# A graph attention layer on one core: ScalarE loads fifteen gathered chunks row by row, six rows with each group of sums

## The chip, the core and the metric

The kernel runs on one core of one Trainium2 chip. A core has five engines, each with its own queue of instructions that it works off in order: TensorE (PE in the profile; its weight loads are PEld), VectorE (DVE), ScalarE (ACT), GpSimd (POOL) and SyncE (SP), which here only issues transfers. They meet through semaphores. Transfers between the chip's memory and the core's on-chip memory (SBUF, 128 partitions) are issued by SyncE, ScalarE or GpSimd and carried out by 16 DMA engines. TensorE writes to PSUM, the accumulator memory. The metric is the device time of one execution in microseconds (us).

## The reference, cut to what matters

```python
h = jnp.maximum(_layernorm(x, axis=-1), 0.0)            # 12500 nodes x 128
# 200000 edges (src, dst), sorted by dst; 4 heads of 32
hn = (h @ W_node.T).reshape(num_nodes, H, HD)
e = (edge_attr_64 @ W_edge.T).reshape(num_edges, H, HD)
att_in = jnp.concatenate([hn[src], hn[dst], e], axis=-1)
att = jnp.sum(att_in * a, axis=-1)
att = jnp.where(att > 0, att, 0.2 * att)
m = jnp.maximum(jax.ops.segment_max(att, dst, num_segments=num_nodes), 0.0)
ex = jnp.exp(att - m[dst])
denom = segment_sum(ex, dst) + (num_edges - deg)[:, None] * jnp.exp(-m)
w = ex / denom[dst]
return x + segment_sum(w[:, :, None] * hn[src], dst).reshape(num_nodes, 128)
```

For each edge the transformed row of its source node is needed. That is the gather on which this document turns: 200000 rows of 137 numbers, 548 bytes each.

## The kernel before, in words

**Stages.** First the nodes are normalised and multiplied by the weights; the rows go to a table in the chip's memory (137 numbers a node: four heads of 32 with a one each, a count, four source logits). Then the edges are worked through in order of their targets.

**Tiling of the edges.** A *chunk* is 128 edges, one a partition. A *group* is four chunks: 511 edges and one place (partition 0 of chunk 0) that carries the sums of the group before. A *quad* is four groups, sixteen chunks. There are 392 groups and 98 quads. Quads are bundled into supers (two quads each at first, then four, then three and two at the end), and the softmax is done once for a super.

**Gathers.** `gather` (L136 to L149) issues one indirect DMA a chunk on GpSimd (L147): 128 rows of the table at 128 source indices, into `ga`. `ga_all` (L130) is a ring of eight quads, so the gathers of quad q need the sums of quad q - 8 to be closed. Quads 0 to 3 and half of quad 4 are gathered from the raw input `x` while the table is still being made.

**By-row chunks.** For some quads the last chunk of the last group is not gathered by GpSimd. `by_row` (L133) lists them: quads 16, 24, ... 96, eleven in all. For these `loaded_by_row` (L701 to L724), a generator that other code steps through, has ScalarE issue 128 small transfers of one row each, into a tile of its own. The source indices come in by a small load (`sources_of`), VectorE scales them to byte addresses (L713), and `windows` (L494) loads sixteen of these addresses at a time into ScalarE's registers (L496). Then come the row transfers (L722). When the logits of that quad are opened, ScalarE copies the tile into `ga` (in `all_logits`, L859).

**The chain of groups.** `sums` (L783) does the following for each group. VectorE weighs the gathered rows (L804) and marks which target each edge has (L817); TensorE multiplies chunks 1 to 3 (L822). Then `complete` closes the *previous* group by `complete_group` (L740 to L763), which is the place of the change:

1. VectorE multiplies the previous group's carried sums into partition 0 of `ga` (L745, the carry);
2. ScalarE copies the carried count (L749, the count copy);
3. the row generator is stepped;
4. TensorE multiplies chunk 0 and so closes the sums (L751);
5. ScalarE copies the closed sums out of PSUM (L752, the copy `pt`);
6. the row generator is stepped again.

The next carry (L745) waits for that copy. One step of the generator issues three rows or one in turn (it pauses ahead of rows p with p % 4 equal to 0 or 3), so a group sends three rows behind the count and one behind the sums, from the first quad on; 1408 rows take 352 groups. The load of the next sixteen addresses stands in the step behind the sums.

**Beside it.** The logits of quads further on (`open_logits`, `all_logits`; L556 to L565) and the softmax of the next super are interleaved with the sums. SyncE fetches the edge features (`ea`), targets (`db`), windows of target logits (`pw`) and of inputs (`xw`) ahead, and writes the results. `add_sources` (L586) is the first to need all gathers of a quad.

Of the kernel before, what the change touches and what calls it, by code (L numbers as in the profile page):

```python
# [15 lines left out]
P = 128  # L16
# [8 lines left out]
R_CNT, R_SRC, ROW = H * HW, H * HW + 1, H * HW + 5  # L25

J = 4
# [4 lines left out]
QG = 4  # L32
# [4 lines left out]
AT_ONCE = 4  # L37
RAW, MORE = 4, 2
QUADS = 8
AHEAD, EVERY = 16, 8  # L40
SETS = max(NODE_T, QG * J)
PAD = 1 << 20

# [1 line left out]
def blocks(total, step):  # L45
    return [(i, min(step, total - i)) for i in range(0, total, step)]
# [3 lines left out]
def kernel(  # L50
# [35 lines left out]
    nc = tc.nc  # L86
# [8 lines left out]
    table = dram.tile([NP, ROW], F32, name="table")  # L95
# [27 lines left out]
    quads = blocks(G, QG)  # L123
    nq = len(quads)
# [5 lines left out]
    ga_all = consts.tile([P, QUADS, QG, J, ROW], F32, name="ga")  # L130
    GA, GATHERED = {}, set()
    whole = lambda g: E - g * NE + 1 >= GE
    by_row = [q for q in range(AHEAD, nq, EVERY) if quads[q][1] == QG and whole(quads[q][0] + QG - 1)]  # L133
    is_by_row = lambda q, i, j: q in by_row and (i, j) == (QG - 1, J - 1)

    def gather(q, rows, width, lo, hi):  # L136
# [26 lines left out]
    with tc.manual_schedule():  # L163
# [6 lines left out]
        for _ in range(AT_ONCE):  # L170
            q, i = early.pop(0)
# [301 lines left out]
    with tc.tile_pool(name="work", bufs=2) as work, \  # L473
# [20 lines left out]
        def windows(of, size, g, n, engine=mybir.EngineType.SP):  # L494

            return nc.values_load_multi_w_load_instructions(  # L496
                of[0:1, g:g + n], engines=[engine], min_val=0, max_val=(N - 1) * size,
                skip_runtime_bounds_check_because="a node's row")[1]

        as_bytes = lambda d: d.bitcast(U8)  # L500
        rows_at = lambda d, at, size, n=SPAN: as_bytes(d.rearrange("n c -> (n c)"))[
            bass.ds(at, n * size)].rearrange("(n c) -> n c", c=size)
# [196 lines left out]
        ROW_TILES = {}  # L699

        def loaded_by_row():  # L701

            def sources_of(q):
                g = quads[q][0] + QG - 1
                of = work.tile([1, P], I32, name="of")
                nc.sync.dma_start(of, src.rearrange("(o e) -> o e", o=1)[:, (g + 1) * GE - P:(g + 1) * GE])
                return of

            of = sources_of(by_row[0]) if by_row else None
            yield  # L710
            for k, q in enumerate(by_row):
                at_row = work.tile([1, P], I32, name="at_row")
                nc.vector.tensor_scalar(at_row, of, float(4 * ROW), None, op0=OP.mult)  # L713
                tile_q = work.tile([P, ROW], F32, name="by_row")
                for p0 in range(0, P, QG * J):
                    if p0 == P // 2 and k + 1 < len(by_row):
                        of = sources_of(by_row[k + 1])
                    at = windows(at_row, 4 * ROW, p0, QG * J, mybir.EngineType.Activation)
                    for p in range(QG * J):
                        if p % J in (0, J - 1):  # L720
                            yield
                        nc.scalar.dma_start(as_bytes(tile_q[p0 + p:p0 + p + 1, :]),  # L722
                                            rows_at(table, at[p], 4 * ROW, 1))
                ROW_TILES[q] = tile_q  # L724

        row_steps = loaded_by_row()
        next(row_steps)

# [3 lines left out]
        def complete():  # L732

            division = None if "held" in state else state.pop("division", None)
            if begun:
                complete_group(*begun.pop())
            if division:
                divide(*division)

        def complete_group(q, i, ga, hot, pt, acc, fc):  # L740
            g0, m = quads[q]
            g = g0 + i
            if g:
                before = state["before"]
                nc.vector.tensor_tensor(  # L745
                    ga[0:1, i, 0, 0:H * HW].rearrange("p (h w) -> p h w", w=HW),
                    before[WIN:WIN + 1, 0:H * HW].rearrange("p (h w) -> p h w", w=HW),
                    fc.unsqueeze(2).to_broadcast([1, H, HW]), op=OP.mult)
                nc.scalar.copy(ga[0:1, i, 0, R_CNT:R_CNT + 1], before[WIN:WIN + 1, R_CNT:R_CNT + 1])  # L749
                next(row_steps, None)  # L750
            nc.tensor.matmul(acc, hot[:, i, 0, :], ga[:, i, 0, :], start=False, stop=True)  # L751
            nc.scalar.copy(pt[:, i, :], acc)  # L752
            state["before"] = acc
            next(row_steps, None)

            parts = {nq - 1: (2, 3), nq - 2: (2,), nq - 3: (2,)}.get(q, ())
            if i + 1 in parts or i == m - 1:
                lo = max([k for k in parts if k <= i], default=0)
                den = work.tile([SPAN, QG, H], F32, name="den")
                nc.scalar.activation(den[:, lo:i + 1, :], pt[0:SPAN, lo:i + 1, R_SRC:R_SRC + H],  # L760
                                     AF.Exp, scale=-1.0)
                state["division"] = q, pt, den, lo, i + 1
# [413 lines left out]
```

## Time and profile before

| | |
|---|---|
| median of 3 runs | 2010.57 us (2009.75 to 2010.74) |
| the profiled execution | 2015.4 us, span 2013.6 us from first to last instruction |
| mean granted TensorE clock | 0.54 |
| bytes moved | 279.70 MB, mean 139 GB/s |

Times of single instructions come from that one profiled execution. In the profile a line of a group gives the source line, the engine, the operation, the tile written and read, the count, then the busy time and the mean duration, then the idle time of the engine just ahead of these instructions and what ended it. A line of the timeline gives the start and the length in us, and in brackets the idle time ahead with its releaser. A line of waits gives who waited, for whom, how long in all, how often, and the longest. ACTq and SPq are the queues of ScalarE and SyncE: issuing a DMA there keeps the queue, but is not counted as busy time of the engine.

### The profile page before, as it was taken

The numbers are of one execution on the slowest core, as the hardware profiler recorded it, in microseconds if no ns is written. First come the engines' busy times: TensorE is split into PE (matmuls) and PEld (weight loads), VectorE is DVE, ScalarE is ACT, GpSimd is POOL, SyncE is SP. The second block draws the span as 40 slices with busy tenths as digits, with TensorE's granted clock in tenths as the row PEclk, the third lists the DMA queues.
The fourth block names the chain that finished last, engine by engine and source line by source line (L and its number), as shares of the span: only waits on it lengthen the run. The fifth ranks groups of instructions, "written<-read, shape, count | busy, mean of one in ns | idle before, by whom it ended". The sixth has DMA issues, their size and how long they took to land. (4 is left out here: it accounts for less than half of the span.)

```text
span 2013.6 us, 30145 instructions
## 1 busy us (share of the span) xinstructions
PE 1383.0 (69%) x7317; PEld 1253.6 (62%) x7317; DVE 1323.0 (66%) x3272; ACT 420.1 (21%) x1542; POOL 1500.1 (74%) x1598
## 2 busy tenths in 40 slices
PE   6587798775766666657666666667575766777775
PEld 5576788765665556656656565566565655666665
DVE  7674788774775766656747655657476565677776
ACT  6664112111111111111111111111111111122122
POOL 7777677777777777777777777777777777777774
PEclk8766555555555555555555555555555555555557
DMA  7654666655566555555555555565555554555541
GB/s 252 204 145 110 156 157 155 162 138 129 134 151 147 133 131 138 135 132 142 128 133 134 136 131 147 122 146 124 136 133 135 133 145 121 138 153 138 134 102 36
DMA packets 196601, 279.70 MB, mean 139 GB/s; under 512 B 81092, under 2 KB 145999, under 8 KB 188584
## 3 DMA queue, kind: packets, MB, share of 16 engines
q1 hardware_dynamic: 142150, 165.56, 30.5%
q0 software_dynamic: 49760, 108.84, 24.0%
q10 hardware_dynamic: 4514, 3.36, 0.7%
q8 instruction: 61, 1.00, 0.2%
q14 instruction: 116, 0.95, 0.2%
HBM read 254.25 MB, written 23.30 MB: 138 GB/s over the span
## 5 line engine op out<-in xcount | busy, mean ns | idle before, releaser
L147 POOL DMA_INDIRECT ga<-table,srci x1483 | 1412.9, 953 | 463.5 <-issue 386.4
L822 PE MATMUL acc<-ga,hot 128*97 128x137 f32 x2352 | 644.8, 445 | 67.9 <-ACT ga L797 29.8
L822 PEld LDWEIGHTS acc<-ga,hot 128*97 128x97 f32 x2352 | 513.3, 276 | 89.0 <-ACT ga L797 48.1
L562 PEld LDWEIGHTS <-at 80*128 80x128 bf16 x1568 | 213.2, 164 | 483.6 <-DVE at L556 465.1
L562 PE MATMUL lg<-pw,at 80*128 80x12 bf16 x1568 | 169.3, 181 | 409.5 <-DVE at L556 405.4
L565 PE MATMUL lg<-wblk,ea 128*128 128x8 f32 x1568 | 407.2, 357 | 0.0
L565 PEld LDWEIGHTS lg<-wblk,ea 128*128 128x128 f32 x1568 | 379.7, 307 | 0.0
L586 DVE TENSOR_TENSOR U<-st,ga 128x64 f32<-128x64 f32 x98 | 26.4, 269 | 413.4 <-DMA ga<-table,srci 403.3
L556 DVE TENSOR_TENSOR at<-const_ps,db 80x512 bf16<-80x512 f32 x392 | 267.3, 683 | 5.8
L804 DVE TENSOR_TENSOR ga<-ga,ex_ps 128x528 f32<-128x528 f32 x392 | 268.4, 685 | 0.6 <-issue 0.3
L751 PE MATMUL acc<-ga,hot 128*97 128x137 f32 x784 | 257.4, 431 | 3.8 <-ACT ga L749 3.7
L752 ACT COPY pt<-acc 97x137 f32<-97x137 f32 x392 | 107.4, 274 | 717.1 <-PE acc L751 655.4
L745 DVE TENSOR_TENSOR ga<-acc,facs 1x132 f32<-1x132 f32 x391 | 115.8, 296 | 132.3 <-ACT pt L752 122.2
L751 PEld LDWEIGHTS acc<-ga,hot 128*97 128x97 f32 x784 | 197.7, 281 | 6.6 <-ACT ga L749 6.5
L817 DVE TENSOR_TENSOR hot<-const_ps,slot 128x320 f32<-128x320 f32 x384 | 183.2, 477 | 0.0
L749 ACT COPY ga<-acc 1x1 f32<-1x1 f32 x391 | 59.9, 153 | 430.6 <-DVE ga L745 408.3
L147 POOL DMA_INDIRECT ga<-in_x_dram,srci x72 | 68.8, 956 | 23.4 <-issue 17.7
L845 DVE TENSOR_TENSOR res<-pt,const_ps 80x512 f32<-80x512 f32 (+2 forms) x102 | 67.5, 662 | 3.8 <-DVE const_ps L841 0.3
L849 DVE TENSOR_TENSOR res<-res,xw 80x512 f32<-80x512 f32 (+2 forms) x99 | 66.8, 675 | 3.4
L404 PE MATMUL row_ps<-wcat,hT 128*128 128x137 f32 x198 | 40.9, 358 | 20.5 <-DVE tgt L410 10.7
L624 ACT ACTIVATE low<-t_ps 64x511 f32<-64x511 f32 (+2 forms) x28 | 16.5, 589 | 176.3 <-PE t_ps L622 176.3
L678 PE MATMUL ex_ps<-ident,ex 64*128 64x64 f32 (+2 forms) x112 | 18.5, 313 | 49.1 <-ACT ex L665 49.1
(139 smaller groups left out, 1045.1 us busy)
## 6 DMA issues: line engine op xcount, KB each, us to landing
db<-in_dst_dram SPq DMA_DIRECT2D x98, 640.0 KB
ea<-in_edge_t_dram SPq DMA_DIRECT2D x98, 512.0 KB
ga<-table,srci POOLq DMA_INDIRECT x1483
by_row<-table ACTq DMA_DIRECT2D x1408, 0.5 KB
xw<-in_x_dram SPq DMA_DIRECT2D x392, 40.0 KB
out_dram<-res SPq DMA_DIRECT2D x392, 40.0 KB
pw<-side SPq DMA_DIRECT2D x392, 1.9 KB
table<-row SPq DMA_DIRECT2D x9, 616.5 KB
```

The costliest lines, as they stand in the source:

```text
L147: nc.gpsimd.indirect_dma_start(out=ga[:, i, j, 0:width], out_offset=None, in_=rows, in_offset=bass.IndirectOffsetOnAxis(ap=srci[:, g0 + i, ...
L556: nc.vector.tensor_tensor(at[:, i, :], node_ps[0:SPAN, g0 + i:g0 + i + 1].to_broadcast([SPAN, GE]), db[:, i, :], op=OP.is_equal)
L562: nc.tensor.matmul(lg[:, i, j].rearrange("p k h -> p (k h)"), at[:, i, j * P:(j + 1) * P], sw, start=i + j == 0, stop=False, skip_group_ch ...
L565: nc.tensor.matmul(lg[:, i, 2 * w:2 * w + 2, 0, :], ea[:, i, w, :], wblk, start=False, stop=True, skip_group_check=True)
L745: nc.vector.tensor_tensor(ga[0:1, i, 0, 0:H * HW].rearrange("p (h w) -> p h w", w=HW), before[WIN:WIN + 1, 0:H * HW].rearrange("p (h w) -> ...
L751: nc.tensor.matmul(acc, hot[:, i, 0, :], ga[:, i, 0, :], start=False, stop=True)
L752: nc.scalar.copy(pt[:, i, :], acc)
L804: nc.vector.tensor_tensor(val, val, weight.unsqueeze(3).to_broadcast([P, J, H, HW]), op=OP.mult)
L817: nc.vector.tensor_tensor(hot[:, i, :, 0:SPAN], lane_ps.unsqueeze(1).to_broadcast([P, J, SPAN]), slot[:, g, :].unsqueeze(2).to_broadcast([ ...
L822: nc.tensor.matmul(acc, hot[:, i, j, :], ga[:, i, j, :], start=j == 1, stop=False)
L845: nc.vector.tensor_tensor(res[:, :n, :].rearrange("p g (h d) -> p g h d", d=HD), val[:, :, :, 0:HD], share_ps[0:R, :n, :].unsqueeze(3).to_ ...
L849: add.tensor_tensor(res[:, :n, :], res[:, :n, :], xw, op=OP.add)
```

## The change

`by_row` is set from other constants, the generator yields after every row, and `complete_group` steps it five times behind the count and once behind the sums, from quad 6 on. The addresses are loaded twelve at a time. The fifteen by-row quads are 21, 26, 31, 37, 42, 47, 53, 58, 63, 69, 74, 79, 85, 90 and 95.

```diff
-AHEAD, EVERY = 16, 8
+ROWS_FROM, ROWS_AHEAD = 6, 9
+BEHIND_COUNT, BEHIND_SUMS, LOADED = 5, 1, 12
...
-    by_row = [q for q in range(AHEAD, nq, EVERY) if quads[q][1] == QG and whole(quads[q][0] + QG - 1)]
+    by_row = [ROWS_FROM + ROWS_AHEAD - -(k + 1) * P // ((BEHIND_COUNT + BEHIND_SUMS) * QG) for k in range(nq)]
+    by_row = [q for q in by_row if q < nq and quads[q][1] == QG and whole(quads[q][0] + QG - 1)]
...
-                for p0 in range(0, P, QG * J):
-                    if p0 == P // 2 and k + 1 < len(by_row):
+                for p in range(P):
+                    if p == P // 2 and k + 1 < len(by_row):
                         of = sources_of(by_row[k + 1])
-                    at = windows(at_row, 4 * ROW, p0, QG * J, mybir.EngineType.Activation)
-                    for p in range(QG * J):
-                        if p % J in (0, J - 1):
-                            yield
-                        nc.scalar.dma_start(as_bytes(tile_q[p0 + p:p0 + p + 1, :]),
-                                            rows_at(table, at[p], 4 * ROW, 1))
-                ROW_TILES[q] = tile_q
+                    if p % LOADED == 0:
+                        at = windows(at_row, 4 * ROW, p, min(LOADED, P - p), mybir.EngineType.Activation)
+                    nc.scalar.dma_start(as_bytes(tile_q[p:p + 1, :]),
+                                        rows_at(table, at[p % LOADED], 4 * ROW, 1))
+                    if p == P - 1:
+                        ROW_TILES[q] = tile_q
+                    yield
+
+        def load_rows(q, n):
+
+            for _ in range(n if q >= ROWS_FROM else 0):
+                next(row_steps, None)
...
                 nc.scalar.copy(ga[0:1, i, 0, R_CNT:R_CNT + 1], before[WIN:WIN + 1, R_CNT:R_CNT + 1])
-                next(row_steps, None)
+                load_rows(q, BEHIND_COUNT)
             nc.tensor.matmul(acc, hot[:, i, 0, :], ga[:, i, 0, :], start=False, stop=True)
             nc.scalar.copy(pt[:, i, :], acc)
             state["before"] = acc
-            next(row_steps, None)
+            load_rows(q, BEHIND_SUMS)
```

## The prediction

> **What bounds the kernel now.** I read the page's busy shares and costliest groups first, then GpSimd's own instructions in order of time, then who waits for whom, stage by stage.
>
> ```profile
> span 2013.6 us, 30145 instructions
> PE 1383.0 (69%) x7317; PEld 1253.6 (62%) x7317; DVE 1323.0 (66%) x3272; ACT 420.1 (21%) x1542; POOL 1500.1 (74%) x1598
> L147 POOL DMA_INDIRECT ga<-table,srci x1483 | 1412.9, 953 | 463.5 <-issue 386.4
> L147 POOL DMA_INDIRECT ga<-in_x_dram,srci x72 | 68.8, 956 | 23.4 <-issue 17.7
> ```
>
> No engine looks full: GpSimd (POOL) leads with 74%. Its busy time is the issue of 1483 + 72 = 1555 indirect gathers, one per 128 edges; the question is what its idle quarter is.
>
> ```profile
> 1009.55 0.94 POOL L147 DMA_INDIRECT ga<-table,srci  x1 [0.30 <-issue]
> 1010.79 0.94 POOL L147 DMA_INDIRECT ga<-table,srci  x1 [0.30 <-issue]
> ...
> 1969.23 0.94 POOL L147 DMA_INDIRECT ga<-table,srci  x1 [0.30 <-issue]
> ```
>
> The gathers stand back to back, 1.25 us from start to start: 0.94 of work and 0.30 that belongs to no wait. Who released GpSimd between 260 us and its last gather, and the group of these gathers, say the same for the whole stretch:
>
> ```profile
> POOL ga L147 <- issue: 354.7, 1163, 0.3
> POOL ga L147 <- PE acc L822: 29.9, 98, 0.3
> POOL ga L147 <- DMA ga<-table,srci: 14.6, 48, 0.3
> L147 POOL DMA_INDIRECT ga<-table,srci x1360 | 1296.3, 953 | 414.7 <-issue 354.7 <-PE acc L822 29.9 <-DMA ga<-table,srci 14.6
> ```
>
> The longest "wait" is 0.3 us whatever its releaser, so these are the fixed gap and no waits. One gather costs (1296.3 + 414.7) / 1360 = 1.258 us, and for 1360 gathers in a row nothing else sets GpSimd's pace. VectorE stands on the other side of that bound:
>
> ```profile
> L586 DVE TENSOR_TENSOR U<-st,ga x38: 266/267/325, 1018.9 to 1760.6; 128x64 f32<-128x64 f32 x38
>   DMA ga<-table,srci: 211.5, 33
> ```
>
> From 1000 to 1780 us L586, which needs a whole quad's gathers, waits 211.5 us for them over 38 quads: 5.6 us a quad in which VectorE, and what follows it, has nothing to do. That is the **cover** for anything the change adds to the group chain. Before 260 us it is different:
>
> ```profile
> POOL ga L147 <- PE acc L751: 11.2, 5, 5.8
> 255.73 0.94 POOL L147 DMA_INDIRECT ga<-table,srci  x1 [5.76 <-PE acc L751]
> ```
>
> From 150 to 260 us GpSimd waits five times for the closing matmul of an old group (L751), which frees a buffer of gathered rows: 11.2 - 5 x 0.3 = 9.7 us that it loses. After its last gather, 2013.6 - 1969.2 = 44.4 us of softmax, sums and results remain.
>
> **The change part by part.** *Fewer gathers.* Eleven by-row chunks become fifteen (the by-row quads are 21, 26, 31, 37 and so on to 95), so 1555 gathers become 1551. Four gathers at 1.258 us: -5.0 us. All lie ahead of GpSimd's last gather, so where they stand does not matter while GpSimd is the bound; the tail behind it keeps its length.
>
> *No rows for quads 0 to 5.* ScalarE used to issue rows from the first sums on, in the stretch where GpSimd waits for L751.
>
> ```profile
> 164.83 2.46 ACTq L722 DMA_DIRECT2D by_row<-table  x3
> 164.96 0.78 PE L751 MATMUL acc<-ga,hot 128*97 128x137 f32 x2
> 167.33 0.27 ACT L752 COPY pt<-acc 97x137 f32<-97x137 f32 x1 [2.42 <-DMA db<-in_dst_dram]
> ...
> ACT pt L752 <- DMA by_row<-table: 8.5, 4, 3.2
> ```
>
> Here three rows hold ScalarE for 2.46 us, and the copy of the sums starts 167.33 - 165.74 = 1.6 us after its matmul. The last row counts such copies from 150 to 256 us: 8.5 us of idle time behind rows in four cases. About 1.0 us of each is the issue itself (below), so 4.5 us are stalls; I take a little over half of that as lying on the way to the groups that GpSimd waits for: -2.5 us. Bounds: 0, and -9.7 if all of GpSimd's waits vanish. A loss is excluded here, since nothing is added to this stretch.
>
> *Six rows a group instead of four, from quad 6.* The place matters: after the count copy L749 ScalarE issues rows, and only then may it copy the closed sums (L752), for which VectorE's next carry (L745) waits.
>
> ```profile
> 1007.81 0.15 ACT L749 COPY ga<-acc 1x1 f32<-1x1 f32 x1 [0.36 <-DVE ga L745]
> 1007.88 0.92 ACTq L722 DMA_DIRECT2D by_row<-table  x3
> 1009.39 0.66 PE L751 MATMUL acc<-ga,hot 128*97 128x137 f32 x2
> 1010.09 0.27 ACT L752 COPY pt<-acc 97x137 f32<-97x137 f32 x1 [2.13 <-PE acc L751]
> 1010.17 0.23 ACTq L722 DMA_DIRECT2D by_row<-table  x1
> 1010.40 0.30 DVE L745 TENSOR_TENSOR ga<-acc,facs 1x132 f32<-1x132 f32 x1 [0.90 <-ACT pt L752]
> ...
> L752 ACT COPY pt<-acc 97x137 f32<-97x137 f32 x160 | 43.8, 274 | 298.2 <-PE acc L751 265.4 <-DMA by_row<-table 26.1 <-PE acc L822 5.7
> ```
>
> Three rows take 0.92 us, so one takes (0.92 - 0.23) / 2 = 0.34 us, and a burst of three is done 1.0 us after L749. ScalarE's idle time ahead of L752 (1000 to 1780 us) is 298.2 / 160 = 1.86 us a group; a DMA issue does not count as busy, so 1.0 of it is the rows and 0.86 is free. Two more rows need 0.69 and fit in the mean: 0.17 stays. The cover for them is the time that L751 takes to come through TensorE's queue behind the next group's L822.
>
> *The register loads.* The row addresses now come in twelves, and their load stands inside the burst behind the count; before, sixteen were loaded behind the single row after the sums.
>
> ```profile
> L496 SPq TENSOR_LOAD <-base_row x98: 294/300/570, 139.6 to 1965.0; - x98
> L496 ACTq TENSOR_LOAD <-at_row x88: 1197/1306/1477, 154.0 to 1840.1; - x88
> ```
>
> Four registers take 0.300 us and sixteen 1.306, so twelve are between; on the line through both, an estimate, 0.300 + 8 x 0.0838 = 0.97 us. A chunk takes 11 loads over 128 / 24 = 5.33 quads, 2.06 a quad, and each overshoots the 0.17 by 0.80: 1.65 us a quad that VectorE's carry may come later. For a load hidden in another wait the price is nothing, without any free time 0.97 x 2.06 + 0.69 x 4 = 4.8 us a quad; I keep 1.65.
>
> *Waits of the rows themselves.* In the built program's order each row DMA waits for one of eight semaphores that rows and SyncE's transfers take in turn, that is for the DMA eight places earlier. Behind a row that waits stand L752, the next count copy and so VectorE's carry.
>
> ```profile
> db<-in_dst_dram SPq DMA_DIRECT2D x98, 640.0 KB
> ea<-in_edge_t_dram SPq DMA_DIRECT2D x98, 512.0 KB
> by_row<-table ACTq DMA_DIRECT2D x1408, 0.5 KB
> xw<-in_x_dram SPq DMA_DIRECT2D x392, 40.0 KB
> out_dram<-res SPq DMA_DIRECT2D x392, 40.0 KB
> pw<-side SPq DMA_DIRECT2D x392, 1.9 KB
> ACT pt L752 <- DMA by_row<-table: 49.4, 26, 3.2
> 1011.20 1.09 ACTq L722 DMA_DIRECT2D by_row<-table  x2
> ```
>
> With 98 each of `ea` and `db`, SyncE issues 3.5 transfers a group; with four rows the eight semaphores last 1.07 groups, with six 0.84. So more rows will wait, SyncE's transfers too, but these are fetched two quads ahead. Today 49.4 us of idle time stand behind rows, in 26 cases with 1.0 us of issue each: 23 us of stall for 1408 rows, 0.017 us a row. The upper end is the pair at 1011.20, 1.09 us where two take 0.57: 0.26 us a row, 6.2 us for the 24 rows of a quad. I take 1 us a quad (0.04 a row), near the low end, because the mean over 1408 rows is a better guide than one pair. Together 1.65 + 1 = 2.65 us a quad against the cover of 5.6: hidden, price nothing, and VectorE's wait at L586 shrinks to about 3 us a quad. If that cover were gone, 80 quads times the excess would come on top.
>
> *Small additions* hidden in the same cover: four more copies of a by-row tile on ScalarE, four more scalings of addresses on VectorE and four small loads of sources on SyncE. Rows end at the sums of quad 85, before that of 87, so the tail has none in either kernel.
>
> **Sum.** -5.0 - 2.5 = -7.5 us. The profiled execution took 2015.4 us with a span of 2013.6, the median of the runs is 2010.57; so span 2006.1, execution 2007.9, and median **2003.1 us**.
>
> **The rivals.** *A: the transfers are the bound, and the rows only change their queue: no change, 2010.6 us.*
>
> ```profile
> 400.00:1000.00 600.00, 394.52 (x2063) 358.44 (x2063) 379.76 (x874) 93.11 (x380) 454.88 (x476) 0.51 0.56 136
> ```
>
> The DMA engines are busy for 0.56 of this stretch, and GpSimd's gap stays 0.30 us whoever released it; if landings set the pace, the gap would vary. The same 128 rows still have to be moved, which speaks for A. The Trainium skill, "DMA: Bandwidth & Descriptors", section "Issuing engines are not separate DMA queues", says that all queues run on the same 16 DMA engines and that a second issuing engine saves only the sequencer's time, usually small beside the transfer; by that rule A holds and the sum would be 0. The trace disagrees on "small": the issue is the bound.
>
> *B: ScalarE's bursts become the bound: slower.* VectorE's carry waits for L752, L752 for the burst. The cover is 5.6 us a quad for 80 quads; what exceeds it piles up, and some is caught up after the rows end:
>
> ```profile
> DVE U L586 <- DMA ga<-table,srci: 21.6, 7, 6.5
> ```
>
> (from 1780 to 1970 us). B decides from the point where 80 x (e - 5.6) exceeds 21.6 + 7.5, that is e = 5.96 us a quad, or (5.96 - 1.65) / 24 = 0.18 us of stall a row. A little above, at 0.19: e = 6.2, 49 - 21.6 - 7.5 = +20 us, so 2030 us. For it: the pair at 0.26 and the shorter turn of the semaphores. Against it: the mean of 0.017 would have to grow tenfold.
>
> *C: GpSimd's early waits stay as they are*, because softmax, not rows, holds L751 there: -5.0 alone, 2005.6 us. The wait at 255.73 comes after a softmax, which speaks for it; the stalls at 164.83, ahead of that softmax, against it.
>
> **How the numbers follow.** Forecast 0.52, C 0.23, A 0.10, B 0.15. A difference of 0.2% (4.0 us) is about what a measurement of this kernel can tell from no change. Forecast and C together (0.75) span -4 to -12 us, A's edge reaches 2010: the range is 1998.5 to 2010. Faster by over 0.2%: forecast and C without a small part of C that falls short, 0.73. Within 0.2%: A and that part, 0.12. Slower: B, 0.15.
>
> **What would show it.** Right: 1551 gathers still back to back at 1.258 us with a longest gap of 0.3 after 260 us; fewer than 9.7 us of waits for L751 ahead of it; L586 still waiting, some 3 us a quad; last gather some 7 us earlier, the same 44 us behind it. Wrong for B: L586 hardly waits, copies L752 released by rows, gaps of several us between gathers or a longer tail. Wrong for A: the gather's interval grows. My sum fails if rows stall by more than 0.18 us each, or if the early waits grow.

## The result and the profile after

| | kernel before | changed kernel |
|---|---|---|
| median | 2010.57 us (2008.40 to 2011.14, 5 runs) | 1998.58 us (1996.38 to 2002.01, 5 runs) |
| ratio, 95% interval | | 0.9945 [0.9931, 0.9960] |
| profiled execution | 2015.4 us, span 2013.6 | 1997.9 us, span 1996.0 |

The change saves 12.0 us by the medians, where 7.5 were forecast (2003.1 us, range 1998.5 to 2010): the measured time lies 0.1 us inside the lower edge of the range. Two repeats beside other kernels, told below, saved 10.3 us (0.9949 [0.9935, 0.9963]) and 10.4 us (0.9940 [0.9923, 0.9958]). The two profiled executions differ by 17.6 us of span, because the one of before lay 4.8 us above its median; times below are medians where there are any. Lines of code after the change stand seven lower from L740 on (the count copy is L756, the closing matmul L758, the copy `pt` L759, the carry L752), two lower for the gather (L149), U (L588) and the address loads (L498).

From the page of the changed kernel:

```profile
span 1996.0 us, 31234 instructions
PE 1391.1 (70%) x7317; PEld 1250.7 (63%) x7317; DVE 1324.6 (66%) x3276; ACT 420.3 (21%) x1546; POOL 1493.7 (75%) x1594
L149 POOL DMA_INDIRECT ga<-table,srci x1479 | 1405.5, 950 | 451.3 <-issue 387.5
L759 ACT COPY pt<-acc 97x137 f32<-97x137 f32 x392 | 107.4, 274 | 1002.7 <-DMA by_row<-table 550.1
```

Shares of busy time hardly move. What moves is idle time: ScalarE's idle time ahead of the copy `pt` is 1002.7 us, and its main releaser is now a row, not the closing matmul.

GpSimd's waits for the closing matmul from 150 to 260 us (us in all, times, longest):

```profile
POOL ga L149 <- PE acc L758: 1.0, 2, 0.7
```

11.2 us of waiting for the closing matmul have become 1.0, of which 0.6 is the fixed gap of two gathers. The group of the gathers from 260 to 1990 us, and the last gather in the timeline:

```profile
L149 POOL DMA_INDIRECT ga<-table,srci x1348 | 1281.1, 950 | 411.0 <-issue 353.7 <-PE acc L829 27.8 <-DMA ga<-table,srci 16.5
```

```profile
1950.46 0.94 POOL L149 DMA_INDIRECT ga<-table,srci  x1 [0.30 <-issue]
```

A gather costs (1281.1 + 411.0) / 1348 = 1.255 us, as before (1.258). The last one starts 18.8 us earlier than the 1969.23 of before, and 1996.0 - 1951.4 = 44.6 us follow its end (43.4 before). So GpSimd is still the bound, and in this profile the whole gain lies ahead of its last gather. Of the 18.8 us some 4 are no work of the change: its gathers happened to last 950 ns and not 953. In the profiles of the two repeats they last 955 and 953 ns, and the last gather starts at 1955.33 and 1954.70, 13.9 and 14.5 us earlier; four gathers (5.0) and the early waits (9.7 - 0.4 = 9.3) add up to 14.3. VectorE's waits from 400 to 1780 us, of the kernel before and of the changed one:

```profile
DVE U L586 <- DMA ga<-table,srci: 376.2, 60, 10.3
DVE ga L745 <- ACT pt L752: 76.7, 106, 1.8
DVE U L586 <- issue: 1.8, 1, 1.8
```

```profile
DVE ga L752 <- ACT pt L759: 215.7, 158, 5.0
DVE U L588 <- DMA ga<-table,srci: 200.9, 48, 9.5
DVE U L588 <- issue: 26.9, 5, 7.8
```

The wait for a quad's gathers (U), the cover, has shrunk from 376.2 / 69 = 5.45 to 200.9 / 69 = 2.91 us a quad. With the waits at U whose releaser the profile doesn't tell ("issue") it is 5.5 and 3.3 us, and 3.2 and 3.3 in the two repeats. In its place VectorE waits for the copy `pt` at the carry. The change pays for the four gathers out of that cover. The cover isn't even: from 1780 to 1970 us, where VectorE of the kernel before waits 21.6 us for gathers at U, that of the changed kernel hardly does:

```profile
DVE U L588 <- DMA ga<-table,srci: 2.0, 1, 2.0
```

### The profile page after: what moved, and what is told of

Same layout as the page of the kernel before. It is cut to its first block, busy times and chain, and to the rows that moved or that the text cites. A ratio compares the mean times of both kernels' runs of the same rounds, so it can differ in the third digit from the quotient of the medians.

```text
span 1996.0 us, 31234 instructions
## 1 busy us (share of the span) xinstructions
PE 1391.1 (70%) x7317; PEld 1250.7 (63%) x7317; DVE 1324.6 (66%) x3276; ACT 420.3 (21%) x1546; POOL 1493.7 (75%) x1594
## 4 chain that ended last, share of the span: by engine, by line
DVE 23%; DMA 22%; PE 18%; issue 14%; POOL 14%; ACT 5%; ACTq 3%; SPq 1%; DVEq 0%; POOLq 0%
POOL ga L149 13%; DMA ga<-table,srci 10%; PE acc L829 8%; DVE at L558 4%; PE lg L567 4%; DMA by_row<-table 3%; DVE res L856 3%; DMA db<-in_dst_dram 2%; DVE res L852 2%; DMA ea<-in_edge_t_dram 2%; ACTq L722 2%; PE acc L758 2%; DMA pw<-side 2%; DVE ga L752 2%; DVE ga L811 2%
## 5 line engine op out<-in xcount | busy, mean ns | idle before, releaser
L149 POOL DMA_INDIRECT ga<-table,srci x1479 | 1405.5, 950 | 451.3 <-issue 387.5
L759 ACT COPY pt<-acc 97x137 f32<-97x137 f32 x392 | 107.4, 274 | 1002.7 <-DMA by_row<-table 550.1
L752 DVE TENSOR_TENSOR ga<-acc,facs 1x132 f32<-1x132 f32 x391 | 115.8, 296 | 301.5 <-ACT pt L759 288.6
L758 PE MATMUL acc<-ga,hot 128*97 128x137 f32 x784 | 262.9, 438 | 19.4 <-ACT ga L756 18.4
L758 PEld LDWEIGHTS acc<-ga,hot 128*97 128x97 f32 x784 | 191.7, 278 | 37.9 <-ACT ga L756 36.6
L588 DVE TENSOR_TENSOR U<-st,ga 128x64 f32<-128x64 f32 x98 | 26.5, 270 | 237.9 <-DMA ga<-table,srci 202.9
L756 ACT COPY ga<-acc 1x1 f32<-1x1 f32 x391 | 59.9, 153 | 194.6 <-DVE ga L752 186.7
L149 POOL DMA_INDIRECT ga<-in_x_dram,srci x72 | 69.7, 968 | 23.3 <-issue 17.4
L680 PEld LDWEIGHTS ex_ps<-ident,ex 64*128 64x128 f32 (+2 forms) x112 | 13.6, 204 | 68.6 <-ACT ex L667 68.6
L406 PE MATMUL row_ps<-wcat,hT 128*128 128x137 f32 x198 | 39.6, 349 | 20.7 <-DVE tgt L412 10.7
```

Source lines behind the costliest of these rows:

```text
L149: nc.gpsimd.indirect_dma_start(out=ga[:, i, j, 0:width], out_offset=None, in_=rows, in_offset=bass.IndirectOffsetOnAxis(ap=srci[:, g0 + i, ...
L752: nc.vector.tensor_tensor(ga[0:1, i, 0, 0:H * HW].rearrange("p (h w) -> p h w", w=HW), before[WIN:WIN + 1, 0:H * HW].rearrange("p (h w) -> ...
```

## The experiments

The kernels of a set shared one chip and the runs of the kernel before. In the first and third set the kernel before takes 2011 us. In the second it takes 2523 us; that set is told after them.

### First set: where do the 12 us come from?

*The changed kernel again.*

> The changed kernel once more, as the measure for the runs beside it. Both theories: 12 us below the kernel before (ratio 0.994), as already measured. Theory T: 5.0 us of it are the four gathers, the other 7 us GpSimd's early waits for L751 (9.7 us before, under 1 us here). Rival R: the early waits give the 2.5 us that I had put down, and each gather saved is worth more than its 1.26 us, some 2.4 us.

Measured: 2000.77 us, ratio 0.9949 [0.9935, 0.9963].

*Rows from the first quad on, as before, but six a group from quad 6.* In quads 0 to 5 four rows a group are loaded; the by-row quads begin at 17, and the gathers stay 1551.

```diff
-    by_row = [ROWS_FROM + ROWS_AHEAD - -(k + 1) * P // ((BEHIND_COUNT + BEHIND_SUMS) * QG) for k in range(nq)]
+    EARLY = ROWS_FROM * QG * 4
+    by_row = [ROWS_FROM + ROWS_AHEAD - -((k + 1) * P - EARLY) // ((BEHIND_COUNT + BEHIND_SUMS) * QG) for k in range(nq)]
...
-            for _ in range(n if q >= ROWS_FROM else 0):
+            for _ in range(n if q >= ROWS_FROM else min(n, 3)):
```

> The same fifteen chunks and 1551 gathers, but quads 0 to 5 get back their four rows a group (three behind the count, one behind the sums); from quad 6 on six rows. T: the early waits come back, 7 to 9 us of them, and the time is 5 us below before (2005.6, ratio 0.9975). R: 2.5 us come back, 9.5 us below before (2001, ratio 0.9953).

Measured: 2006.13 us, ratio 0.9976 [0.9966, 0.9986], 5.4 us above the changed kernel beside it. GpSimd's waits from 150 to 260 us are back:

```profile
POOL ga L150 <- PE acc L759: 7.4, 3, 5.8
```

That is 7.4 - 0.9 = 6.5 us against 0.4 in the changed kernel. The rows in the first six quads do cause the early waits, and leaving them out is worth about the waits themselves.

*Four of the fifteen chunks gathered as well.* The rows are still loaded, but GpSimd gathers four of these chunks too and the gathered rows are used; 1555 gathers, and four loaded tiles are not read.

```diff
-    is_by_row = lambda q, i, j: q in by_row and (i, j) == (QG - 1, J - 1)
+    again = by_row[2:14:3]
+    is_by_row = lambda q, i, j: q in by_row and q not in again and (i, j) == (QG - 1, J - 1)
...
-            if q in by_row:
+            if q in by_row and q not in again:
```

> All fifteen chunks are loaded by rows as in the changed kernel, but four of them (the third, sixth, ninth and twelfth) are gathered by GpSimd as well and the loaded tile is not read: 1555 gathers, as before the change. T: 4 x 1.26 = 5.0 us longer than the changed kernel, 7 us below before (2003.6, ratio 0.9965). R: 9.5 us longer than the changed kernel, 2.5 us below before (2008, ratio 0.9988).

Measured: 2006.59 us, ratio 0.9974 [0.9964, 0.9985], 5.8 us above the changed kernel. Four gathers are worth 5.8 us by the medians, 5.0 by the sum; the interval is wide enough for both. In the profiles the last gather starts at 1960.40 instead of the 1955.33 of the changed kernel in this set, 5.1 us later. GpSimd's early waits are as small as in the changed kernel.

*Four rows a group from quad 6, sixteen addresses a load*: ten chunks, 1556 gathers.

```diff
-BEHIND_COUNT, BEHIND_SUMS, LOADED = 5, 1, 12
+BEHIND_COUNT, BEHIND_SUMS, LOADED = 3, 1, 16
```

> Four rows a group as before the change (three and one, sixteen addresses a load), but from quad 6 on: ten chunks, 1556 gathers, one more than before. T: the early waits go, 9 us, and one gather comes back, 1.25: 7 to 8 us below before (2003, ratio 0.9963). R: 2.5 less 1.25 to 2.4, within 1 us of before (2010, ratio 1.000).

Measured: 2005.14 us, ratio 0.9969 [0.9956, 0.9981], although it has one gather more than the kernel before. Its waits (GpSimd from 150 to 260 us, then VectorE from 400 to 1780 us):

```profile
POOL ga L149 <- PE acc L758: 0.6, 2, 0.3
```

```profile
DVE U L588 <- DMA ga<-table,srci: 372.7, 58, 10.9
DVE ga L752 <- ACT pt L759: 75.8, 100, 1.8
```

The early waits are gone and the cover is that of before: the late start gives 5.9 us although it has to pay for one more gather, so 7.1 by itself. The rival, by which the late start is worth 2.5 us and a gather 2.4, expected 1.000 here and falls. Of the 10 to 12 us, 5 to 6 come from the four gathers and the rest from the early waits. That six rows a group cost nothing is shown less sharply: from this kernel to the changed one five gathers go, 6.3 us by the sum, but the medians differ by 4.4, and the tail behind the last gather is 1.1 us longer (44.9 against 43.8 us). Each ratio is known to about 2.6 us, so a price of some 2 us isn't excluded.

### Third set: how much of the cover is left?

*The changed kernel beside the next three.*

> The changed kernel beside the three that follow. On a chip on which the kernel before takes about 2011 us: ratio 0.995 as in the two measurements so far. On a chip like that of the last four runs, where the kernel before took 2523 us and register moves of 0.03 us on ScalarE and SyncE often take 0.7 us: GpSimd is not the bound there (its gathers waited for buffers), so theory T has no ground, each row costs at ScalarE, and the ratio is that of the kernel with sixteen addresses a load, 1.012.

Measured: 2000.61 us, ratio 0.9940 [0.9923, 0.9958].

*Seven rows a group, fourteen addresses a load*: 17 chunks, 1549 gathers. A third tile for the by-row chunks lets loading run one chunk further ahead.

```diff
-BEHIND_COUNT, BEHIND_SUMS, LOADED = 5, 1, 12
+BEHIND_COUNT, BEHIND_SUMS, LOADED = 6, 1, 14
...
-                tile_q = work.tile([P, ROW], F32, name="by_row")
+                tile_q = work.tile([P, ROW], F32, name="by_row", bufs=3)
```

> Seven rows a group, 17 chunks, 1549 gathers. Where GpSimd is the bound: theory T gives -2.5 us against the changed kernel (ratio 0.993), as four more rows a quad take 1.25 of the 2.9 us a quad of wait at U that are left. Rival B: the rows' own waits double from 0.12 us, the cover is spent, +10 us or more against the changed kernel (ratio 1.000 or above), waits at U near 0. Where ScalarE's and SyncE's sequencers are held: about 1.4% above the changed kernel, as it stood to the kernel with sixteen addresses a load (2579 against 2545 us).

Measured: 2103.21 us, ratio 1.0445 [1.0423, 1.0468], 102.6 us above the changed kernel with two gathers fewer. VectorE's waits from 400 to 1780 us, of the changed kernel in this set and of seven rows:

```profile
DVE ga L752 <- ACT pt L759: 216.8, 160, 5.4
DVE U L588 <- DMA ga<-table,srci: 215.3, 51, 10.2
DVE run L674 <- ACT fac L672: 22.4, 18, 3.4
```

```profile
DVE ga L752 <- ACT pt L759: 466.0, 197, 6.7
DVE run L674 <- ACT fac L672: 38.1, 16, 5.0
DVE den L843 <- ACT den L767: 19.4, 13, 5.5
```

No wait at U is left: the cover is spent. The carry waits 249 us more, the two other waits on ScalarE, at `run` and `den`, 29 us more; over the 66 quads of that stretch that is 4.2 us a quad, against some 3.2 that were there to be used. GpSimd now waits for buffers (from 260 to 1990 us), and the tail behind its last gather is 2101.4 - 2012.6 = 88.7 us, where the changed kernel in this set has 46.0:

```profile
POOL ga L149 <- PE acc L758: 82.9, 60, 6.3
```

```profile
2011.68 0.94 POOL L149 DMA_INDIRECT ga<-table,srci  x1 [0.30 <-issue]
```

The last gather starts 57.0 us later than the 1954.70 of the changed kernel, and the tail grows by 42.7: a late VectorE shows in both places, since GpSimd may run eight quads ahead before it has to wait. Which part of the bursts grew was not what rival B said. The rows' own waits (worked out from the trace: ScalarE's idle time between a row's register move and its issue, less the 0.04 us of a row that waits for nothing) are 220 us for 2139 rows, 0.10 us a row against 0.13 in the changed kernel. The address loads are the larger part (their durations in ns, least, median and longest; the changed kernel, then seven rows):

```profile
L498 ACTq TENSOR_LOAD <-at_row x165: 718/1058/1147, 265.3 to 1806.4; - x165
```

```profile
L498 ACTq TENSOR_LOAD <-at_row x170: 661/1546/3559, 265.0 to 1881.7; - x170
```

Grouped by their place in the chunk, the medians over 17 chunks are:

```
first address of the load:  0    14    28    42    56    70    84    98   112   126
median ns:               1498  3336  1508  3334  1507  3331  1504  3325  1535   780
```

Every second load of fourteen takes 3.33 us instead of 1.50. Those that begin at a multiple of 28 are the short ones. All loads sum to 367 us against 168, 199 us more; the four rows more a quad are 4 x 0.34 = 1.4 us, some 106 us over 78 quads. Both together are 305 us where the cover is 3.2 x 78 = 250. That sum leaves 55 us, VectorE's waits 4.2 - 3.2 = 1.0 us a quad or 78 us, and 105 were measured with the two gathers; the order of size is explained, the rest isn't. This kernel changes the rows, the loads and a buffer at once, so what rows alone would cost isn't separated.

*Each load of addresses written twice.*

```diff
                     if p % LOADED == 0:
+                        windows(at_row, 4 * ROW, p, min(LOADED, P - p), mybir.EngineType.Activation)
                         at = windows(at_row, 4 * ROW, p, min(LOADED, P - p), mybir.EngineType.Activation)
```

> Each load of twelve addresses issued twice, rows and result unchanged: 2.0 us a quad more in ScalarE's bursts. Where GpSimd is the bound: theory T, within 3 us of the changed kernel (ratio 0.995), waits at U down to about 60 us over 69 quads. Rival: stretches of softmax have no wait at U to spare and pass the addition on, 10 us or more above the changed kernel (ratio 1.000 or above). Where the sequencers are held: about 1.1% above the changed kernel (2573 against 2545 us).

Measured: 2059.48 us, ratio 1.0234 [1.0215, 1.0252], 58.9 us above the changed kernel. It is not the experiment that was meant. The trace has 165 loads, as many as the changed kernel:

```profile
L498 ACTq TENSOR_LOAD <-at_row x165: 717/989/1078, 267.8 to 1871.4; - x165
```

Where the added load should stand there is a semaphore increment of about 0.02 us: the program that ran has no loads whose registers nobody reads. Rows, loads and all other work are the same, and TensorE, ScalarE, GpSimd and SyncE have the same operations in the same order but for semaphore instructions; on VectorE five of 3281 stand elsewhere. What else differs is the semaphore that a transfer takes: 821 of ScalarE's 1931 DMAs and 525 of SyncE's 1443 take another one, so rows stand behind other transfers. The rows' own waits, reckoned as above, are 473 us for 1881 rows, 0.25 us a row against 0.13; behind the targets `db` 166 us against 74, behind the results 108 against 26. One such burst, with the transfer that it waits for, in the timeline of this kernel (the carry is L753 here, the count copy L757, the copy `pt` L760):

```profile
1007.50 0.15 ACT L757 COPY ga<-acc 1x1 f32<-1x1 f32 x1 [0.36 <-DVE ga L753]
1008.22 0.32 SPq L315 DMA_DIRECT2D db<-in_dst_dram  x1
1008.66 6.70 ACTq L723 DMA_DIRECT2D by_row<-table  x5
...
1015.40 0.27 ACT L760 COPY pt<-acc 97x137 f32<-97x137 f32 x1 [7.74 <-DMA by_row<-table]
1015.70 0.30 DVE L753 TENSOR_TENSOR ga<-acc,facs 1x132 f32<-1x132 f32 x1 [6.50 <-ACT pt L760]
```

SyncE issues `db`, 640 KB, at 1008.22; in five rows of 6.70 us, where five without a wait take 1.6, one stands until that has landed, and VectorE's carry waits 6.50 us. VectorE's waits from 400 to 1780 us:

```profile
DVE ga L753 <- ACT pt L760: 455.6, 225, 7.1
```

Again nothing is left at U; the carry waits 239 us more, 3.5 us a quad. The tail is 94.8 us, 48.8 longer, and the last gather starts 14.5 us later. So longer waits of the rows are enough to spend the cover: that is rival B's mechanism, at 0.25 us a row, with the same rows and the same loads. That the five moved instructions of VectorE have no part in it is argued from the size of these waits and not tested.

*Three rows behind the count and three behind the sums.*

```diff
-BEHIND_COUNT, BEHIND_SUMS, LOADED = 5, 1, 12
+BEHIND_COUNT, BEHIND_SUMS, LOADED = 3, 3, 12
```

> Six rows a group, three behind the count and three behind the sums, 1551 gathers. Where GpSimd is the bound and only the number of rows matters: the changed kernel's time, ratio 0.995. If the place matters: waits at U below 100 us over 69 quads and up to 5 us more, ratio 0.997. Where the sequencers are held: about 0.5% above the changed kernel (2557 against 2545 us).

Measured: 2011.30 us, ratio 1.0003 [0.9989, 1.0017], 10.7 us above the changed kernel, more than either expectation. ScalarE's waits behind rows from 400 to 1780 us, of the changed kernel in this set and of three and three:

```profile
ACT pt L759 <- DMA by_row<-table: 478.3, 179, 5.1
```

```profile
ACT pt L759 <- DMA by_row<-table: 217.4, 103, 4.3
ACT hot L782 <- DMA by_row<-table: 178.0, 51, 6.3
```

The waits of `pt` are halved, but the rows behind the sums hold the copy that opens the next quad (L782) and the divisors `den`. VectorE's waits in the same stretch, of three and three:

```profile
DVE ga L752 <- ACT pt L759: 231.8, 139, 7.8
DVE U L588 <- DMA ga<-table,srci: 147.2, 28, 9.1
DVE den L843 <- ACT den L767: 40.1, 55, 1.8
```

It waits 40.1 us for `den` instead of 5.8, and the cover at U falls from 215.3 to 147.2 us. By that mean the addition would still be hidden, but the cover isn't even. The last long wait for gathers at U ends at 1726.02 us, 1.2 us later than a wait at U of the same quad ends in the changed kernel (1724.86). From there on next to no wait is left that could absorb a delay, and the U of the last quad starts 11.5 us later than the 1962.29 of the changed kernel:

```profile
1973.83 0.25 DVE L588 TENSOR_TENSOR U<-st,ga 128x64 f32<-128x64 f32 x1
```

Between the two, from 1730 to 1970 us, VectorE waits 11.4 us longer at the carry, `run` and `den` (55.8 against 44.4). The last gather starts only 3.5 us later, at 1958.16, and 53.6 us follow its end instead of 46.0. The place of the rows matters, and behind the count is the better one.

### Second set: another thing is the bound

The same three kernels, and the changed kernel with sixteen addresses a load (`LOADED` 16 instead of 12), ran where the kernel before takes 2522.93 us (2503.27 to 2531.46, 9 runs) at nearly the same granted clock (0.53). This set and the third, which ran some 18 minutes later, carry the same chip number, 6 (the first has 8). So whether it was another chip, or one chip at another time, isn't known, and what is said of chips in the expectations is an assumption.

> The changed kernel with sixteen addresses a load instead of twelve: 8 loads a chunk of 1.31 us instead of 11 of about 0.97, so 10.5 against 10.7 us of loads a chunk. Theory T (GpSimd is the bound, the size of a load is hidden): the changed kernel's time, ratio 0.995. Rival: the longer single load overshoots the free time in a burst by more (1.31 - 0.17 = 1.14 against 0.80, 8 against 11 times: 9.1 against 8.8 us a chunk), which is no difference either; only a ratio off by more than 0.002 would show that the place of the loads matters.

> Seven rows a group (six behind the count), fourteen addresses a load, three tiles for by-row chunks; 17 chunks, 1549 gathers. Theory T (GpSimd is the bound, the cover holds): from four rows a group to six VectorE's wait at U for gathers fell from 372.7 to 200.9 us over 69 quads, 2.5 us a quad for 8 rows. Four more rows a quad at that price take 1.25 of the 2.9 us a quad that are left; two gathers less give -2.5 us against the changed kernel: ratio to the kernel before 0.993. Rival B (ScalarE's bursts become the bound): the row's own waits went from 0.02 to 0.12 us when eight rows a quad were added; if they double again, 28 x 0.24 + 1.4 of issue is 5.2 us a quad over today's 2.9 of waits and the cover of 2.9 is spent: 80 x 0.3 or more, +10 us and up against the changed kernel, ratio 1.000 or above, waits at U near 0, gaps of several us between gathers or a longer tail.

> Each load of twelve addresses is issued twice, rows and result unchanged. 2.06 loads a quad at some 0.97 us each: ScalarE's bursts are 2.0 us a quad longer, against 2.9 us a quad of wait at U. Theory T (the cover of 2.9 us a quad holds on the mean): the time of the changed kernel within 3 us, ratio 0.995, waits at U down from 200 to about 60 us over 69 quads. Rival (the cover isn't where it is needed: stretches of softmax without any wait at U pass on what is added): the buffers come free late there, GpSimd waits for L758, and the run is 10 us or more above the changed kernel, ratio 1.000 or above.

> Still six rows a group, 24 a quad, fifteen chunks and 1551 gathers, but three behind the count and three behind the sums. If only the number of rows matters (cover of 2.9 us a quad), the time is the changed kernel's, ratio 0.995. If the place matters: behind the count 0.86 us a group were free before L759, while rows behind the sums stand ahead of ScalarE's other work (exponentials, copies of logits) and of the next count copy; then the waits at U fall below 100 us over 69 quads, and the time rises by up to 5 us, ratio 0.997.

Measured: sixteen addresses 2544.81 us, ratio 1.0120 [1.0071, 1.0169]; seven rows 2579.38 us, 1.0219 [1.0178, 1.0261]; loads written twice 2573.36 us, 1.0199 [1.0148, 1.0250]; three and three 2557.44 us, 1.0146 [1.0104, 1.0188]. GpSimd's waits of the first from 260 to 2500 us, and the register moves ahead of the rows (least, median and longest in ns):

```profile
POOL ga L149 <- remote: 203.3, 93, 3.2
POOL ga L149 <- PE acc L758: 163.3, 38, 23.3
```

```profile
L722 ACTq MOVE by_row<-table x1920: 2/29/1409, 397.8 to 2320.7; - x192
```

GpSimd waits for buffers in every stretch, so it is not the bound, and no theory of this document has its ground there: "remote" is a releaser that the trace doesn't show. A register move of 29 ns takes up to 1.41 us; 95 of ScalarE's 1922 and 170 of SyncE's 1180 take over 0.3 us, and none does in the changed kernel of the third set. Gathers, copies and matmuls last as long as elsewhere. These four ratios say that each of the four kernels costs 1.2 to 2.2% in that condition; they don't say anything about the cover, and what held the queues up stays open. The changed kernel itself wasn't run in this set. Whether sixteen addresses a load are better than twelve where the kernel before takes 2011 us stays open.

## Why the prediction was right

The bound, the direction and the cover were right. The sum was 4.5 us short of the first measurement and some 3 us short of the repeats, most of it in one term, and one of the terms that held did so by luck.

**Fewer gathers, -5.0: right.** The gather's interval stayed at 1.255 us, and four gathers added back cost 5.8 us.

**No rows for quads 0 to 5, -2.5: the mis-sized term.** It was taken as a little over half of 4.5 us of stalls. In the trace the 9.7 us that GpSimd lost became 0.4, and two experiments (rows from the first quad on; four rows a group) put the late start at 5.4 and 5.9 us by the medians, the second with one gather more. The upper bound, -9.7, was on record. The 4.5 us were too few: they come from the four copies whose last releaser was a row. Where a row stood behind a transfer of SyncE, the same view books the wait under that transfer (the kernel before, 150 to 256 us):

```profile
ACT pt L752 <- DMA db<-in_dst_dram: 2.4, 1, 2.4
ACT ga L749 <- DMA out_dram<-res: 1.4, 1, 1.4
ACT pt L752 <- DMA out_dram<-res: 1.4, 1, 1.4
ACT hot L775 <- DMA pw<-side: 1.0, 1, 1.0
```

The rows' own waits in this stretch, reckoned as above, are 8.3 us, and none of these waits is left in the changed kernel. Whether the time of the rows' issue lies on the chain as well there, no run separates. The kernel before has two copies at 164.12 and 167.33, the second shown in the prediction; here is the first, and then the changed kernel at the same place:

```profile
164.12 0.27 ACT L752 COPY pt<-acc 97x137 f32<-97x137 f32 x1 [0.87 <-PE acc L751]
```

```profile
163.38 0.27 ACT L759 COPY pt<-acc 97x137 f32<-97x137 f32 x1 [0.86 <-PE acc L758]
163.69 0.29 DVE L752 TENSOR_TENSOR ga<-acc,facs 1x132 f32<-1x132 f32 x1 [2.23 <-ACT pt L759]
164.02 0.15 ACT L756 COPY ga<-acc 1x1 f32<-1x1 f32 x1 [0.36 <-DVE ga L752]
164.22 0.78 PE L758 MATMUL acc<-ga,hot 128*97 128x137 f32 x2
165.04 0.27 ACT L759 COPY pt<-acc 97x137 f32<-97x137 f32 x1 [0.86 <-PE acc L758]
```

Without rows the second copy starts as soon as its matmul is done, 1.66 us after the first one instead of 3.21. Such steps add up until the groups on which GpSimd waited are closed in time.

**Six rows, the loads and the rows' waits, together 2.65 us a quad, hidden: right in the sum, partly by luck.** The cover fell by 5.45 - 2.91 = 2.54 us a quad (2.2 with all waits at U), and U still waits the forecast 3 us. But the rows' own waits grew from 0.02 to 0.13 us a row, where 0.04 was taken: 0.13 x 24 = 3.1 us a quad instead of 1. With 1.65 for the loads the prediction's own sum would have been 4.8, and under 1 us of cover left. The carry waited 215.7 - 76.7 = 139 us more, 2.0 us a quad; so part of these stalls fell into time in which the copy would have waited for its matmul anyway. How much, no run separates; that it made up for the stalls that were priced too low wasn't foreseen. A load of twelve took 1.06 us (0.97 estimated). One stall in the changed kernel, of the kind that was priced too low:

```profile
1238.97 0.32 SPq L315 DMA_DIRECT2D db<-in_dst_dram  x1
...
1245.47 0.23 ACTq L722 DMA_DIRECT2D by_row<-table  x1
1245.75 0.22 ACT L782 CAST hot<-is_last 128x16 f32<-128x16 bf16 x1 [4.25 <-DMA db<-in_dst_dram]
```

**The tail: nearly right**, 44.6 us behind the last gather, against 43.4; 44.9 and 46.0 in the repeats. So 1 to 3 us of the gain ahead of the last gather are lost behind it. The cover that is spent from 1780 us on fits that, but no run shows it to be the cause.

**The rivals.** *A, the transfers as the bound,* falls: the gather's interval didn't grow, and gathers taken away or added move the time by what their issue costs. By the rule of the Trainium skill, "DMA: Bandwidth & Descriptors", section "Issuing engines are not separate DMA queues", the time saved by issuing elsewhere is usually small beside the transfer; these runs don't agree, 1.255 us of issue a gather being the bound, while the packets of a gather keep the 16 DMA engines busy for 0.31 us (24.0% of the span before, over 1555 gathers). *C, early waits unchanged,* falls with the 1.0 us left of 11.2. *B, ScalarE's bursts as the bound,* didn't come about, but it was nearer than its 0.15 says. It was put at 0.18 us of stall a row; the changed kernel has 0.13, and the program with 0.25 is 58.9 us slower. So the point lies between these two, as forecast, but its slope was too steep: by the prediction's formula 0.25 us a row is 80 x (7.65 - 5.6) - 29.1 = 135 us above the kernel before, and 48.5 were measured. The distance to the point was wrong, since the price of a row's wait was a mean over the 1408 rows of the kernel before. The turn of the semaphores, shorter with six rows by the prediction's own working (0.84 groups instead of 1.07), may be why more rows stand behind SyncE's transfers; that isn't shown, since with seven rows the turn is shorter still (0.76) and a row waits 0.10 us, less than with six.

No version that ran in the first and third sets is faster than the changed kernel.

## What to carry to other kernels

Price an edit against the idle time of the engine that has to wait for it, stage by stage: here the same rows were free, to within some 2 us, from quad 6 on, where VectorE had 5.45 us a quad to spare on the mean, and cost 5 to 7 us in the first quads, where GpSimd itself waited. Look at the stretch where the cover is thinnest, not at its mean: with three rows behind the count and three behind the sums 147 us of it were left, and the gain was gone, because none was left behind 1726 us. A transfer that is issued between two steps of a chain can hold that chain until another one that shares its completion semaphore has landed (some 5 us of the burst at 1008.66), so count who shares them before more small transfers go in. When cover is left, say how much and what spends it: one row a group more, with its awkward loads, turned -10 us into +92 against the kernel before.

## What the runs showed of the hardware

- **Loads of registers depend on count and place.** Sixteen addresses took 1.31 us in the kernel before and 1.20 in the one with four rows from quad 6, twelve 1.06; fourteen took 1.50 or 3.33 in turn, as they began at an even or an odd multiple of fourteen.
- **Another assignment of semaphores went with 2.9% more time**: 2059.48 against 2000.61 us with the same rows, loads and arithmetic, some 165 increments of 0.02 us more, and the rows' own waits at 0.25 instead of 0.13 us a row.
- **The same kernel took 2011 us in two sets and 2523 us in another**, at granted clocks of 0.54 and 0.53; in the latter register moves on ScalarE took up to 1.41 us instead of 0.03. Whether that goes with the chip or the time, and what holds them, is open.
